# Three small edits to the routing and the last norm of a two-layer decoder kernel

## The chip, the cores and the metric

The kernel runs on one core of one Trainium2 chip. The metric is the device time in microseconds (us) of one execution; times of before and after are medians of several executions. A core has five engines that run side by side, each through its own queue in order: TensorE (PE; PEld is its weight load), VectorE (DVE), ScalarE (ACT), GpSimd (POOL) and SyncE (SP). DMA transfers are issued from the queues of SP, ACT and POOL.

## The reference, cut to what matters

Two decoder layers over 16 batches of 128 tokens with 512 features: a state-space scan, cross-attention, a ternary feed-forward, ternary self-attention, a gated cross-attention, and a mixture of experts. Each sub-layer is added to its input and normed:

```
x = _layernorm(x + _L1_xattn_ref(x, ctx_2048, ...))
x = _layernorm(x + _L1_ffn_ref(x, ...))
```

The change lies in the last one. For each token the router computes softmax scores over 64 sub-experts and keeps the top 8; these lie in 8 groups of 8. For each group with a chosen sub-expert, the token gets a mix of the group's mask vectors added, goes through the group's gate, up and down projections, and the result is scaled by the sum of its weights in the group and added up over the groups:

```
xg = x[:, None, :] + einsum('ngi,ghi->ngh', soft, mask_up_w)
a = silu(einsum('ngh,gih->ngi', xg, gate_proj_w)) * einsum('ngh,gih->ngi', xg, up_proj_w)
y = einsum('ng,ngh->nh', scalar, einsum('ngi,ghi->ngh', a, down_proj_w))
```

## The kernel before, in words

Five stages follow one another: the scan, cross-attention, feed-forward, attention (self and gated) and the experts. Tokens are held on chip as 16 tiles k.x[b] of 128 x 512.

**Order of the work.** The code is written with the Tile layer: it traces instructions in the order in which the Python code runs, and a planner then fixes each engine's queue. It goes by written order, but lets an instruction move ahead as soon as, in its own estimate of times, its inputs and its buffer are ready. On the chip a queue is then run in order: an instruction that waits holds all behind it. `k.tc.keep_in_program_order(ins)` ties an instruction behind the one that was traced just before it on the same engine; it holds back that instruction only. A tile with a tag shares its tag's buffers: with bufs=4, the fifth one waits until the first has been read for the last time.

**Routing.** `Moe.route(p)` routes the pair of batches 2p and 2p+1. It is a generator whose pieces (up to each `yield`) are set between other work by `tick()`, twice in each step of the loop. In order: transpose x (L1413), copy to r_x (L1415), scores (L1420), softmax (L1427), top 8, sorting by group through a matmul with `sel` (L1449), group sums `scal`, exponentials r_ex (L1460), counts by matmul (L1467); then places, and the routing rows. A row is 776 numbers a token: 512 of x (the copy in L1476, on ACT), 256 of the group weights (L1498 and L1499, on DVE), 8 of `scal` (L1500). Rows have four buffers, two pairs' worth. Then `scatter` stores each row to DRAM (L1507, on SP) and sends it to the buckets of its groups with indirect DMAs (L1509, on POOL), two in each step: 16 for a pair of the first half, 14 for one of the second. Batches 0 to 7 (pairs 0 to 3) are routed within the gated attention, pairs 4 to 7 from the third step of the expert stage on.

**Experts.** `stage_moe` runs over 98 units: two halves, 8 groups, 6 tiles of 128 bucket rows each, and for the last group of the second half the 8 batches 8 to 15 themselves. In step t the loop fetches the row of unit t+5 (L1519, SP), and for its neighbours makes the weights' transpose (places: pts, soft), the mask sum xg (L1546, L1548), its transpose (turn_in: ptx L377 through transpose4, copy L1554 on ACT), the gate and up projections (L1562, activation L1565 on ACT, product L1566 on DVE), the transpose of act (L1572, L1574), the down projection (L1579), and the store of the result (L1589, DMA from ACT's queue in L1590). `combine` gathers results back (L1598) and adds them to x (L1605) on POOL. The weights of a group and its mask matrix mup (L1381 to L1391) are loaded ahead.

**The end.** For the last group, `store` adds y to x[b] (L1584); after each odd b it calls `finish(b - 1)`, which norms both batches with one call of `layernorm` (L62): statistics L68 and L69 for each, one chain of eleven small DVE steps for both (`rsqrt`, L53 to L58), a scaling for each (L72), and two stores to DRAM (L1617, SP).

Of the kernel before, what the change touches and what calls it, by code (L numbers as in the profile page):

```python
# [10 lines left out]
F32 = mybir.dt.float32  # L11
# [9 lines left out]
P = 128  # L21
NB = 16
D = 512
# [38 lines left out]
def layernorm(k, ins, outs, eps=1e-5, keep=lambda ins: ins):  # L62

    nc, n = k.nc, len(ins)
    mv = k.small.tile([P, n, 2], F32, tag=f"ln_mv{n}", name="ln_mv")
    for i, r in enumerate(ins):
        st = k.small.tile([P, nc.vector.BN_STATS_DIM], F32, tag="ln_st", name="ln_st")
        keep(nc.vector.bn_stats(st, r))  # L68
        keep(nc.vector.bn_aggr(mv[:, i, :], st))  # L69
    rstd = rsqrt(k, mv[:, :, 1], n, eps, keep=keep)  # L70
    for i, (r, o) in enumerate(zip(ins, outs)):
        keep(nc.vector.tensor_scalar(o, r, mv[:, i, 0:1], rstd[:, i : i + 1], ALU.subtract, ALU.mult))  # L72
# [656 lines left out]
def stage_ffn(k):  # L729
# [4 lines left out]
    with ExitStack() as ctx:  # L734
# [24 lines left out]
        for n, sn in enumerate(states):  # L759
            nxt = prepare(states[n + 1]) if n + 1 < len(states) else iter(())  # L760
            for i, x in enumerate(sn.xs):
                st = sn.step[:, i : i + 1]
                po = po_.tile([P, D], F32, tag="po", name="po")
                for h in range(HB):
# [24 lines left out]
                    if n and h >= 2:  # L789
                        next(ahead, None)  # L790
                nc.vector.tensor_tensor(x, po, x, ALU.add)
            late = finish(sn)
        for _ in late:
            pass
# [520 lines left out]
class Moe:  # L1315
# [90 lines left out]
    def route(self, p):  # L1406

        k, nc, wr, E, NG = self.k, self.nc, self.wr, self.E, self.NG
        half, xs = p // (NB // 4), k.x[2 * p : 2 * p + 2]
# [38 lines left out]
        for i in range(2):  # L1448
            nc.tensor.matmul(pf[:, i], wT[:, i * P : (i + 1) * P], self.sel, start=True, stop=True)  # L1449
        yield  # L1450
        rows = [wr.tile([P, self.ROW], F32, tag="r_row", name="r_row", bufs=4) for _ in range(2)]
        scal = wr.tile([P, 2, NG], F32, tag="r_sc", name="r_sc", bufs=2)
        ind = wr.tile([P, 2, NG], F32, tag="r_in", name="r_in", bufs=2)
        indb = wr.tile([P, 2, NG], BF16, tag="r_ib", name="r_ib", bufs=2)
# [17 lines left out]
        nc.vector.tensor_scalar(s16, s16, 1e-30, None, ALU.max)  # L1472
        nc.vector.reciprocal(s16, s16)
        nc.vector.tensor_tensor(e3, e3, s16.unsqueeze(2).to_broadcast([P, 2 * NG, self.GS]), ALU.mult)
        for x, row in zip(xs, rows):
            nc.scalar.copy(row[:, 0:D], x)  # L1476
        yield
        pos = wr.tile([P, 2, NG], F32, tag="r_po", name="r_po", bufs=2)
        for i in range(2):
            off = wr.tile([P, NG], F32, tag=f"r_off{half}", name="r_off", bufs=2)  # L1480
# [100 lines left out]
    def store(self, u):  # L1581
        if u.to is None:
            b, k = u.b, self.k
            self.nc.vector.tensor_tensor(k.x[b], u.y, k.x[b], ALU.add)  # L1584
            if b % 2:
                self.finish(b - 1)
            return
        y = self.wk.tile([P, D], F32, tag="yo", name="yo", bufs=3)
        self.nc.vector.tensor_copy(y, u.y)  # L1589
        self.nc.scalar.dma_start(u.to, y)  # L1590
# [19 lines left out]
                yield  # L1610
            self.finish(b - 1, k.tc.keep_in_program_order)

    def finish(self, b, keep=lambda ins: ins):
        xs = self.k.x[b : b + 2]
        layernorm(self.k, xs, xs, keep=keep)
        for i, x in enumerate(xs):
            self.nc.sync.dma_start(self.k.args["out"][b + i], x)  # L1617
# [210 lines left out]
```

## Time and profile before

| | us |
|---|---|
| median of 3 executions | 3327.35 (3319.4 to 3329.7) |
| the profiled execution | 3324.17 |
| its span, first to last instruction | 3322.3 |
| PE busy in the span | 3145.9 (95%) |
| DVE, POOL, ACT busy | 1872.8, 1388.4, 1379.3 |
| mean granted TensorE clock | 0.972 of full speed |

The profile gives each instruction of one execution with its engine, line, start and duration. "Idle before" is the time that the engine stood before an instruction, with what it waited for last. The view by stretches gives the busy time of each engine between two times; the view of waits sums who waited for whom (in total, times, longest); the view of a tile lists the instructions that touch it, and what they waited for. A row of the timeline with x2 or more merges neighbours of one form.

### The profile page before, as it was taken

To read this page: it belongs to the slowest core of one execution; us is meant where nothing else is said; L and a number is where in the kernel's file an instruction comes from. 1 tells how busy PE (TensorE), PEld (TensorE's weight loads), DVE (VectorE), ACT (ScalarE), POOL (GpSimd) and SP (SyncE) were. 2 spreads that over 40 slices of the span, in tenths; PEclk is the share of its full clock that TensorE was granted. 3 is DMA by queue.
4 is the path that set the end of the run, shared out by engine and by line. 5 is a ranking of instruction groups with operands and counts; after the bars stand their busy time and mean duration, and the time that the engine had idled before them with its cause. 6 is when DMAs were issued, how large, how long until landed. Compare 5 with 4: busy or idle time off the path is not lost. (4 is left out here: it accounts for less than half of the span.)

```text
span 3322.3 us, 38519 instructions
## 1 busy us (share of the span) xinstructions
PE 3145.9 (95%) x12894; PEld 1811.7 (55%) x12944; DVE 1872.8 (56%) x4202; ACT 1379.3 (42%) x3299; POOL 1388.4 (42%) x1196
## 2 busy tenths in 40 slices
PE   6899998899999999999999989999999999999998
PEld 3444544455555555555566555666655566666665
DVE  5887878556556556556486669765553232233224
ACT  4655555233233233234433379865643231122221
POOL 6978887233333333332100066226624455333331
PEclk8999999999999999999999989999899999999999
DMA  7533332690000000001300010014435566555441
GB/s 235 134 81 97 85 85 69 227 310 8 7 4 4 7 4 4 7 0 76 112 1 1 29 36 1 11 58 150 149 115 185 193 222 210 167 180 175 160 160 62
DMA packets 162577, 317.29 MB, mean 96 GB/s; under 512 B 20233, under 2 KB 83209, under 8 KB 159300
## 3 DMA queue, kind: packets, MB, share of 16 engines
q1 hardware_dynamic: 124164, 216.23, 21.0%
q0 software_dynamic: 19200, 64.18, 5.6%
q10 hardware_dynamic: 19008, 34.35, 2.7%
q8 instruction: 105, 1.72, 0.2%
q14 instruction: 100, 0.82, 0.1%
HBM read 238.80 MB, written 129.04 MB: 111 GB/s over the span
## 5 line engine op out<-in xcount | busy, mean ns | idle before, releaser
L245 POOL TENSOR_TENSOR dBx<-dtx,BC 128x1024 f32<-128x1024 f32 x128 | 301.9, 2379 | 33.3 <-DVE h L258 26.0
L1562 PE MATMUL pg<-gu,xgT 128*128 128x352 f32 x784 | 299.4, 464 | 1.4 <-ACT act L1565 1.4
L1562 PE MATMUL pu<-gu,xgT 128*128 128x352 f32 x784 | 298.6, 463 | 0.1
L1566 DVE SCALAR_TENSOR_TENSOR act<-pu,row,act 128x352 f32<-128x352 f32 x98 | 57.1, 582 | 383.9 <-PE pu L1562 336.1
L1579 PE MATMUL y<-dn,aT 128*128 128x512 f32 x588 | 268.3, 592 | 0.0
L585 POOL TENSOR_TENSOR pr<-pr,sm 128x512 f32<-128x512 f32 x128 | 134.5, 1051 | 289.5 <-DVE sm L584 235.1
L236 ACT ACTIVATE h<-dt,negA 128x254 f32<-128x254 f32 x512 | 239.8, 474 | 14.9 <-DVE dt L178 2.1
L1605 POOL TENSOR_TENSOR x<-got,x 128x512 f32<-128x512 f32 x120 | 152.1, 1273 | 217.2 <-DMA got<-results,gidx 216.8
L616 PE MATMUL po<-w,aT 128*128 128x512 f32 x512 | 230.6, 593 | 0.5 <-DVE aT L610 0.5
L493 PE MATMUL pq<-w,xT 128*128 128x512 f32 x512 | 228.9, 594 | 0.0
L470 POOL TENSOR_TENSOR m<-m,m 128x512 f32<-128x512 f32 x96 | 121.4, 1265 | 245.3 <-DVE m L465 245.3
L1598 POOL DMA_INDIRECT got<-results,gidx x120 | 116.0, 966 | 253.0 <-DMA results<-yo 183.6
L578 ACT ACTIVATE pr<-sc,mx,sf 128x256 f32<-128x256 f32 x256 | 142.6, 561 | 188.1 <-DVE mx L571 175.8
L258 DVE TENSOR_TENSOR_SCAN h<-h,dBx 128x1024 f32<-128x1024 f32 x80 | 183.2, 2294 | 57.6 <-ACT h L236 43.0
L267 PE MATMUL py<-hC,ident 128*128 128x512 f32 x320 | 166.9, 650 | 41.2 <-ACT y L272 36.2
L1562 PEld LDWEIGHTS pu<-gu,xgT 128*128 128x128 f32 x784 | 150.3, 192 | 84.1 <-issue 2.4
L1562 PEld LDWEIGHTS pg<-gu,xgT 128*128 128x128 f32 x784 | 142.8, 192 | 65.8 <-issue 2.8
L1565 ACT ACTIVATE act<-pg 128x352 f32<-128x352 f32 x98 | 45.4, 464 | 299.6 <-PE pg L1562 278.6
L1579 PEld LDWEIGHTS y<-dn,aT 128*128 128x128 f32 x588 | 104.1, 190 | 100.8 <-issue 94.2
L1554 ACT COPY xgT<-ptx 128x512 f32<-128x512 f32 x98 | 57.3, 586 | 230.3 <-PE ptx L377 221.1
L1589 DVE COPY yo<-y 128x512 f32<-128x512 f32 x90 | 62.1, 690 | 156.7 <-PE y L1579 145.7
L493 PEld LDWEIGHTS pq<-w,xT 128*128 128x128 f32 x512 | 93.5, 190 | 102.0 <-issue 99.0
(363 smaller groups left out, 6830.5 us busy)
## 6 DMA issues: line engine op xcount, KB each, us to landing
bucket<-zeros SPq DMA_DIRECT2D x96, 388.0 KB, 8.2
row<-bucket SPq DMA_DIRECT2D x90, 388.0 KB, 3.5
BC<-bcd SPq DMA_DIRECT2D x128, 256.0 KB, 4.9
results<-yo ACTq DMA_DIRECT2D x90, 256.0 KB, 3.2
gu<-in_moe_guT SPq DMA_DIRECT2D x16, 1408.0 KB, 7.4
cT<-in_ctxT SPq DMA_DIRECT2D x32, 256.0 KB, 6.0
dn<-in_moe_downT SPq DMA_DIRECT2D x16, 512.0 KB, 6.8
rows<-r_row SPq DMA_DIRECT2D x16, 388.0 KB, 3.0
```

The lines of the kernel that those rows point to most:

```text
L236: nc.scalar.activation(h[:, c, :, 1:], st.dt[:, c].rearrange("p (b t) -> p b t", b=BQ)[:, :, 1:], AF.Exp, scale=negA[:, c, n : n + 1])
L245: nc.gpsimd.tensor_tensor(dBx, st.dtx, BC[:, 0].unsqueeze(1).to_broadcast([P, KC, TQ]), ALU.mult)
L258: nc.vector.tensor_tensor_scan(hf, hf, df, 0.0, ALU.mult, ALU.add)
L267: nc.tensor.matmul(st.py[c], k.ident, st.hC[n][:, 2 * c : 2 * c + 2], start=n == 0, stop=n == NS - 1)
L470: nc.gpsimd.tensor_tensor(m1, m1, m2, ALU.add)
L493: nc.tensor.matmul(ps, src[:, c], w[c], start=c == 0, stop=c == KC - 1)
L578: nc.scalar.activation(pr[:, j], st.sc[g, i][:, j], AF.Exp, scale=st.sf[:, h : h + 1], bias=st.mx[g, i][:, j : j + 1], accum_out=sm[:, j : ...
L585: nc.gpsimd.tensor_tensor(pr, pr, sm.unsqueeze(2).to_broadcast([P, 2, 2 * P]), ALU.mult)
L616: nc.tensor.matmul(st.po, aT[:, j], k.wo[h // 8][:, h % 8], start=h == 0, stop=h == G * J - 1)
L1562: nc.tensor.matmul(ps, u.xT[:, c], gu[:, c, lo : lo + I], start=c == 0, stop=c == KC - 1)
L1579: self.nc.tensor.matmul(u.y, u.aT[:, c], u.w[1][:, c], start=c == 0, stop=c == 2)
L1605: nc.gpsimd.tensor_tensor(k.x[b], got, k.x[b], ALU.add)
```

## The change

The rows are taken from their pool in the last piece of `route` instead of the third from last; the two copies of x into them are written in that last piece too, behind the `yield` that stood after them, and each is kept in its written place on ACT. The last two batches, 14 and 15, are normed and stored one by one.

```diff
@@ route
-        rows = [wr.tile([P, self.ROW], F32, tag="r_row", name="r_row", bufs=4) for _ in range(2)]
         scal = wr.tile([P, 2, NG], F32, tag="r_sc", name="r_sc", bufs=2)
...
         nc.vector.tensor_tensor(e3, e3, s16.unsqueeze(2).to_broadcast([P, 2 * NG, self.GS]), ALU.mult)
+        yield
+        rows = [wr.tile([P, self.ROW], F32, tag="r_row", name="r_row", bufs=4) for _ in range(2)]
         for x, row in zip(xs, rows):
-            nc.scalar.copy(row[:, 0:D], x)
-        yield
+            k.tc.keep_in_program_order(nc.scalar.copy(row[:, 0:D], x))
         pos = wr.tile([P, 2, NG], F32, tag="r_po", name="r_po", bufs=2)
@@ store
             self.nc.vector.tensor_tensor(k.x[b], u.y, k.x[b], ALU.add)
-            if b % 2:
+            if b >= NB - 2:
+                self.finish(b, n=1)
+            elif b % 2:
                 self.finish(b - 1)
@@ finish
-    def finish(self, b, keep=lambda ins: ins):
-        xs = self.k.x[b : b + 2]
+    def finish(self, b, keep=lambda ins: ins, n=2):
+        xs = self.k.x[b : b + n]
```

## The prediction, made before the change was run

> **What bounds the kernel now.** I read the page's busy times first (TensorE busy 95% of the span), then the busy time of each engine by stage. Columns of a row below: stretch, its length, then PE, PEld, DVE, ACT and POOL busy, the granted clock, DMA share, GB/s. The three stretches are the end of the attention stage, the first routed part of the expert stage, and the rest of it.
>
> ```profile
> 2180.00:2440.00 260.00, 239.60 (x1573) 154.99 (x1572) 156.23 (x521) 167.00 (x516) 131.45 (x126) 0.91 0.31 110
> 2440.00:2660.00 220.00, 205.59 (x815) 127.47 (x816) 80.62 (x203) 64.46 (x129) 83.00 (x77) 0.97 0.55 187
> 2660.00:3300.00 640.00, 640.00 (x2374) 390.19 (x2373) 182.65 (x391) 137.32 (x312) 243.83 (x223) 1.00 0.51 171
> ```
>
> From 2660 us on TensorE has no gap and the full clock, so whatever TensorE loses earlier in this stage moves the end one for one. Between 2440 and 2660 us it loses 14.4 us, and more to the clock. Next I asked the waits of TensorE from 2420 us on, and the view of the tile r_row (the routing rows):
>
> ```profile
> PE ptx L377 <- DVE xg L1548: 9.6, 3, 4.8
> PE pts L1540 <- DMA row<-bucket: 2.5, 3, 1.3
> ```
>
> ```profile
> L1476 ACT COPY r_row<-x x16: 601/618/621, 2190.8 to 2631.7; 128x512 f32<-128x512 f32 x16
> ...
>   DMA bucket<-r_row,r_to: 34.5, 4
> ...
>   DVE x L72: 18.4, 6
> ```
>
> ACT stands still at the copy into a routing row ten times: four times, 34.5 us, until a scatter has read the row buffer that it wants, six times, 18.4 us, until the norm has written x. The timeline shows what the first kind does to TensorE (start, duration, engine, line; idle before in brackets):
>
> ```profile
> 2549.49 0.97 POOL L1509 DMA_INDIRECT bucket<-r_row,r_to  x1 [0.30 <-issue]
> ...
> 2551.39 0.62 ACT L1476 COPY r_row<-x 128x512 f32<-128x512 f32 x1 [9.51 <-DMA bucket<-r_row,r_to]
> 2551.91 0.46 ACT L1565 ACTIVATE act<-pg 128x352 f32<-128x352 f32 x1
> ...
> 2552.91 0.68 DVE L1548 TENSOR_TENSOR xg<-pm,row 128x512 f32<-128x512 f32 x1
> ...
> 2553.73 0.71 PE L377 MATMUL ptx<-ident,xg 128*128 128x128 f32 x4 [4.32 <-DVE xg L1548]
> ...
> 2554.23 1.38 PE L1562 MATMUL pg<-gu,xgT 128*128 128x352 f32 x2
> ...
> 2557.67 0.76 PE L1562 MATMUL pu<-gu,xgT 128*128 128x352 f32 x2
> ```
>
> The row to see is the ACT copy: the activation of the unit (L1565) is queued behind it, DVE's product L1566 and sum L1548 behind that, and TensorE, out of work, idles 4.32 us. Then a pair of matmuls takes 1.38 us instead of 0.76 until 2557.67. The wait table names DVE; the cause is two steps back, on ACT. The second such place:
>
> ```profile
> 2631.72 0.62 ACT L1476 COPY r_row<-x 128x512 f32<-128x512 f32 x1 [11.29 <-DMA bucket<-r_row,r_to]
> ...
> 2634.06 1.09 PE L377 MATMUL ptx<-ident,xg 128*128 128x128 f32 x4 [4.78 <-DVE xg L1548]
> ```
>
> The other two waits (7.79 and 5.90 us) fit into ACT's slack but for 0.72 us of TensorE at 2618.93.
>
> **Part 1, copies kept in their written place: the expert stage.** The two waiting pairs are batches 12 to 15. Their copies sit in ACT's queue some 110 us ahead of the rest of their routing step: the exact part of a row (L1499) is written at 2669.06 and 2730.55. In their written place they come just before that. The buffers they need were last read by scatters issued at 2559.67 and 2628.58 that landed by 2563 and 2632, so they are free by about 100 us: no wait. Gone are 4.32 + 4.78 + 0.72 = 9.8 us of idle TensorE, and the slow matmuls. A pair of matmuls at full clock is 0.59 us from the next (2557.67 to 2558.26; the row's 0.76 overlaps it). First place: three pairs from 2554.23 to 2557.67 take 3.44 instead of 3 x 0.59 = 1.77, 1.7 lost. Second: from 2634.06 to 2639.57, 5.5 us, for four transposes (0.45 at full clock) and four pairs (2.36), 2.7 lost. Together 4.4, and the sum is 14.2 us. The Trainium skill (TensorE: Matmul & The Clock Gate, What's actually happening) has the clock halved after an idle window of about 3.4 us and restored after about 3.4 us of work: that would make 1.7 per stall, 3.4 in all, and 13.2 us. The second row shows a slow stretch of 5.5 us, so I take 14.2.
>
> What is late next: without the block, L1565 follows its matmuls at once and leaves ACT 3.5 us idle before it, as in every undisturbed unit (pitch 8.42 us); nothing else in that stretch is late by more than the 2.5 us of row fetches at 2458 to 2468, which stay. Ends: 12 to 16.
>
> What moves with the copies: they are 16 x 0.62 us on ACT. In the expert stage eight of them (batches 8 to 15) land in ACT's 3.5 us gaps: nothing; without that cover, 2 x 0.52 a routing step, 4 us. Each hangs behind the ACT instruction written before it, mostly the issue of a results store, which waits for DVE's yo; queued behind are only the next unit's ACT steps, 3.5 us away. The row's store on SP and its scatters on POOL need copy and L1499. POOL takes up the scatters of these four steps 10, 4.8, 4.7 and 5.7 us after L1499, so the copy has that long. SP's fetches behind a row store run five units (42 us) ahead. Cost 0.
>
> **Part 1 in the attention stage.** Here the copies of batches 0 to 11 follow the norm at once. Where TensorE feels it: at 2194.18 it waits 1.41 us for at_T (L1042), queued behind two copies, and at 2234.95 1.69 us for at_T behind a copy that had waited 2.31 for the norm. Together some 3 us. At the longest ACT wait (7.89 us to 2279.36) TensorE's three waits name DVE, and DVE stood behind its own wait of 5.50 us for POOL's x (L1232): no gain there. Against it: eight of these copies now fall into the middle of other exps, 8 x 0.52 = 4.2 us of an ACT that is busy 167 of 260 us; I charge about a third of it, 1.3. The order of the whole stage is planned anew around the moved copies. Net gain 2, ends from a gain of 8 (half the 18.4 us turned into TensorE time) to a loss of 6 (all 4.2 us on the path and one slow-clock stretch of 1.7).
>
> Taking the rows later, after the yield, moves no instruction but the row's own writes (L1498 to L1500), which come later than that place anyway, but for L1500, by 3 to 5 us of no consequence: nobody waits for it before L1499. Cost 0; at worst it rides with the copy.
>
> **Part 2, the last two batches.** After the last matmul everything is DVE:
>
> ```profile
> 3309.01 0.16 DVE L56 TENSOR_TENSOR rs_t<-rs_y 128x2 f32<-128x2 f32 x1
> 3309.09 0.69 DVE L1584 TENSOR_TENSOR x<-y,x 128x512 f32<-128x512 f32 x1
> ...
> 3311.53 0.68 DVE L1584 TENSOR_TENSOR x<-y,x 128x512 f32<-128x512 f32 x1
> ...
> 3313.19 0.17 DVE L53 TENSOR_SCALAR rs_a<-ln_mv 128x2 f32<-128x2 f32 x1
> ...
> 3315.36 1.00 DVE L72 TENSOR_SCALAR x<-x,ln_mv,rs_y 128x512 f32<-128x512 f32 x2
> ```
>
> Batch 15 is added at 3311.53; stats and aggregate to 3313.19; eleven small steps, 2.17 us, to 3315.36; two scalings to 3316.36; two stores, the second landing behind the first. Batch 14 was added at 3309.09 and waited for 15. Now 14 gets eleven steps of its own and 15's end carries one scaling less (0.5). The Trainium skill (VectorE: DVE Perf Modes, The DRAIN you can't avoid) speaks against this: the next step starts only when the pipeline is empty, so keep the count of steps low. At the dependent pitch of 0.195 us that is 11 x 0.195 = 2.1 more, less 0.5: 1.6 slower. But the first two rows show a step that doesn't depend on the one before it starting 0.08 later, so 14's steps fit between 15's. Three of them start before 3311.53; the other eight and 14's scaling cost some 0.7 that the gaps don't hide: last scaling ends 0.2 later. The last store then runs alone: stores land in 2.2 to 3.1 us here, I take 0.7 off. Net gain 0.5; ends: gain 1.2 (all in gaps), loss 2.3 (14 wholly ahead of 15).
>
> **Sum.** 14.2 + 2 + 0.5 = 16.7 off a span of 3322.3, 3305.6; with the 1.9 us around it (3324.17 - 3322.3), 3307.5 against 3324.17. The median, 3327.35, lies 3.2 above that execution: 3310.5.
>
> **Rivals.** (a) *The gain goes back into a new order (14 in 100).* The planner fills the freed ACT queue with another early instruction that waits: ACT already waits 12.3 us in five places for the load of mup (L1385), up to 4.0 each. For: it is the same kind. Against: those fit in the 3.5 us slack now. If two of them cost as much as the first stall now (4.3 + 1.7 = 6 us): 3322.5. (b) *The attention stage gains too (12 in 100).* The 18.4 us were felt by half, and its slow clock (0.91) recovers: 8 instead of 2, and 2 more of clock: 3302.5. Against: the waits there name DVE. (c) *Slower (6 in 100).* POOL at the third and fourth routing steps takes up the scatters 0.56 us after L1499 (2337.07, 2337.63; 2377.47, 2378.03). A copy queued late behind exps on ACT would hold POOL there, and with it the attention norms (L1206) and x behind it; the longest such wait now is 5.8. Four steps at 5.8 and a slow clock of 1.7 each make 30 us, less 14.7: 3343. It is slower on balance from 3.7 us a step. Against: ACT has slack, and the copy's input is long ready. (d) That nothing changes would need the 34.5 us to be no cause of TensorE's stalls; the chain of starts 2551.39, 2551.91, 2552.91, 2553.73 leaves no room for that.
>
> **Chances.** Likeliest, 68 in 100, 3303 to 3317; (b) 12, (a) 14, (c) 6. The runs before spread over 10 us, so 0.3% (10 us) is about what can be told from no change: faster by more 0.79, within 0.15, slower 0.06. Range 3300 to 3319: the likeliest case, (b), and the nearer edge of (a).
>
> **What would show it.** Right: no ACT wait for a scatter at L1476; the PE wait for xg down to about 0.5 us; PE busy near 220 of 220 less the 4 to 5 us at the stage's start; copies within 5 us before L1499. Wrong: a new ACT wait in the expert stage, POOL waiting for r_row from ACT, or an attention stage longer by several us. The tail is right if 15's scaling ends within 5.5 us of the last matmul.

## The result, and the profile after

| | before | after |
|---|---|---|
| median of 6 executions each, one comparison | 3328.11 (3319.40 to 3336.66) | 3304.88 (3301.27 to 3308.06) |
| the profiled execution, its span | 3324.17, 3322.3 | 3305.51, 3303.3 |
| mean granted TensorE clock | 0.972 | 0.976 |

The ratio is 0.9934, with a 95% interval of 0.9918 to 0.9950: 23.2 us faster between the medians, 19.0 between the spans. The forecast was 3310.5. Its main term came out nearly as worked out; a second one was some two and a half to four times too small.

First the busy time by stretch, as before the change (length, then PE, PEld, DVE, ACT and POOL busy, granted clock, DMA share, GB/s):

```profile
2180.00:2440.00 260.00, 241.13 (x1620) 156.18 (x1619) 161.67 (x556) 168.33 (x519) 133.63 (x128) 0.94 0.33 113
2440.00:2660.00 220.00, 215.90 (x869) 133.58 (x868) 86.88 (x220) 70.98 (x138) 91.00 (x85) 0.99 0.61 201
2660.00:3290.00 630.00, 630.00 (x2331) 383.64 (x2330) 176.98 (x372) 133.43 (x304) 234.59 (x214) 1.00 0.51 169
```

Two different things have happened. In the second row TensorE stands idle 4.1 us instead of 14.4, and its clock went from 0.97 to 0.99. In the first row the idle time is almost what it was, 18.9 us after 20.4, and yet more matmuls fit into the same 260 us (1620 after 1573), because the clock went from 0.91 to 0.94. The trace holds the clock itself, which is either 1.00 or 0.50: TensorE was at half clock for 47.8 of these 260 us before and for 30.7 after, which is up to 8.5 us of lost time less. The expert stage got back the time of its stalls and of the slow clock behind them; the attention stage got back time of slow clock alone.

TensorE's waits from 2400 us on (in total, times, longest):

```profile
PE pts L377 <- DVE at_T L1044: 4.0, 1, 4.0
PE pts L1540 <- DMA row<-bucket: 1.8, 3, 0.8
PE pg L1562 <- ACT act L1565: 1.4, 1, 1.4
PE ptx L377 <- DVE xg L1548: 0.5, 1, 0.5
```

The wait for xg is down from 9.6 us to 0.5. The view of the tile r_row says why:

```profile
L1477 ACT COPY r_row<-x x16: 612/621/650, 2246.4 to 2717.4; 128x512 f32<-128x512 f32 x16
...
  ACT at_s L1198: 6.4, 1
```

Before, the copies ran from 2190.8 to 2631.7 us; now they run from 2246.4 to 2717.4. The two lines on idle ACT, for a scatter (34.5 us) and for the norm (18.4 us), are gone. What is left is one wait of POOL, 6.4 us, that names ACT. That looks like rival (c), a late copy that holds POOL. The timeline of that place clears it (DVE, ACT and POOL rows of the same kernel):

```profile
2374.87 0.62 ACT L1477 COPY r_row<-x 128x512 f32<-128x512 f32 x1
...
2376.32 0.49 DVE L1499 TENSOR_TENSOR r_row<-r_ex,r_row 128x128 fp32r<-128x128 f32 x2
...
2377.37 1.01 POOL L1509 DMA_INDIRECT bucket<-r_row,r_to  x1 [6.37 <-ACT at_s L1198]
```

The copy ends at 2375.49, the row's exact part at 2376.81, and the scatter follows 0.56 us after that, as it did before (2377.47, 2378.03, after a wait of 5.82). POOL waits for DVE; the exp on ACT that is named merely ended just then. The copy costs nothing there.

The end, with 14 and 15 normed apart:

```profile
3292.86 0.15 DVE L53 TENSOR_SCALAR rs_a<-ln_mv 128x1 f32<-128x1 f32 x1
3292.93 0.68 DVE L1584 TENSOR_TENSOR x<-y,x 128x512 f32<-128x512 f32 x1
...
3294.85 0.28 DVE L56 TENSOR_TENSOR rs_t<-rs_y 128x1 f32<-128x1 f32 x2
3295.04 0.28 DVE L57 SCALAR_TENSOR_TENSOR rs_t<-rs_t,rs_a 128x1 f32<-128x1 f32 x2
...
3296.01 0.54 DVE L72 TENSOR_SCALAR x<-x,ln_mv,rs_y 128x512 f32<-128x512 f32 x1
3297.05 0.55 DVE L72 TENSOR_SCALAR x<-x,ln_mv,rs_y 128x512 f32<-128x512 f32 x1
```

Batch 14's chain begins (3292.86) just as batch 15 is added (3292.93), and the small steps of the two chains lie between each other: the pairs of steps (x2) start 0.19 us apart, no further than the single steps before. The last scaling ends at 3297.60, 5.13 us after the last matmul; before it was 5.22.

### The profile page after: what moved, and what is told of

Its sections match the earlier page's. It is cut to its first block, busy times and chain, and to the rows that moved or that the text cites. A ratio compares the mean times of both kernels' runs of the same rounds, so it can differ in the third digit from the quotient of the medians.

```text
span 3303.3 us, 38574 instructions
## 1 busy us (share of the span) xinstructions
PE 3138.6 (95%) x12944; PEld 1804.4 (55%) x12944; DVE 1876.6 (57%) x4213; ACT 1379.7 (42%) x3299; POOL 1387.5 (42%) x1196
## 4 chain that ended last, share of the span: by engine, by line
PE 68%; DVE 8%; ACT 3%; POOL 1%; issue 1%; DMA 1%; SPq 0%; POOLq 0%; ACTq 0%; DVEq 0%
PE y L1579 7%; PE pu L1562 7%; PE pg L1562 7%; PE pq L493 7%; PE po L616 6%; PE po L783 4%; PE pk L493 3%; PE sc L565 3%; PE ao L605 3%; PE pt L377 3%; PE pv L493 3%; PE ps L1144 2%; PE pu L769 2%; PE pg L769 2%; PE pT L593 1%; PE ptx L377 1%
## 5 line engine op out<-in xcount | busy, mean ns | idle before, releaser
L245 POOL TENSOR_TENSOR dBx<-dtx,BC 128x1024 f32<-128x1024 f32 x128 | 301.7, 2376 | 34.5 <-DVE h L258 27.5
```

Source lines behind the costliest of these rows:

```text
L245: nc.gpsimd.tensor_tensor(dBx, st.dtx, BC[:, 0].unsqueeze(1).to_broadcast([P, KC, TQ]), ALU.mult)
```

## The experiments

The theory: the gain of the expert stage comes from the tie alone, which keeps the copies of batches 12 to 15 from standing in ACT's queue for a buffer that is not free. The rivals: the gain comes from taking rows and writing the copy later, from scarce row buffers, from the tail, or from the attention stage. Each profile gives two stage lengths: the attention stage with routing (first scores of the gated attention to first gate projection of the experts) and the expert stage (first gate projection to last y). "Ratio" is to the kernel before in the same comparison, with its 95% interval; before's median was 3328.11 beside the change, 3328.30 beside e1 to e4, 3324.25 beside e5 to e8 and 3328.14 beside e9 to e12.

| kernel | attention | experts | median | ratio |
|---|---|---|---|---|
| before | 331.7 | 864.8 | 3328.11 | |
| after | 324.8 | 849.8 | 3304.88 | 0.9934 (0.9918 to 0.9950) |
| e1 tail only | 332.5 | 864.6 | 3327.69 | 0.9999 (0.9987 to 1.0010) |
| e2 routing only | 331.1 | 849.7 | 3306.15 | 0.9930 (0.9908 to 0.9953) |
| e3 later, no tie | 332.1 | 866.0 | 3327.05 | 1.0000 (0.9991 to 1.0009) |
| e4 tie only | 334.5 | 850.3 | 3311.70 | 0.9949 (0.9930 to 0.9968) |
| e5 the change again | 324.2 | 849.4 | 3304.21 | 0.9938 (0.9924 to 0.9952) |
| e6 late half tied | 335.3 | 850.0 | 3314.53 | 0.9964 (0.9951 to 0.9977) |
| e7 early half tied | 327.9 | 864.5 | 3317.02 | 0.9975 (0.9964 to 0.9985) |
| e8 change, x on DVE | 305.8 | 849.5 | 3289.22 | 0.9900 (0.9881 to 0.9919) |
| e9 change, two rows | 322.4 | 850.5 | 3304.69 | 0.9938 (0.9923 to 0.9952) |
| e10 before, x on DVE | 318.3 | 867.3 | 3312.75 | 0.9954 (0.9938 to 0.9970) |
| e11 before, filler | 334.3 | 864.8 | 3323.47 | 0.9988 (0.9980 to 0.9995) |
| e12 e8, other turns | 311.2 | 852.2 | 3292.93 | 0.9904 (0.9889 to 0.9918) |

### e1 and e2: the two parts apart

e1 is the kernel before with the tail's edit alone:

```diff
-            if b % 2:
+            if b >= NB - 2:
+                self.finish(b, n=1)
+            elif b % 2:
                 self.finish(b - 1)
```

> The kernel before with the change of the last two batches alone. My account (routing carries the gain, the tail some 0.4 us): median within 3 us of the kernel before, four ACT waits for a scatter at the row copies still there (about 34 us), last scaling ends 5.1 us after the last matmul as against 5.2. Rival (the tail carries several us of the 23): 3318 to 3322 us.

e2 is the change without that edit; its diff is the `route` part of the change.

> The change without its last part: batches 14 and 15 normed as a pair. My account: like the full change within 1 us, 3305 to 3306, with no ACT wait for a scatter. Rival (tail carries several us): 3309 or more.

The tail alone can't be told from no change (12 executions against 23). The routing alone is as fast as the whole change (4 executions, 3299.67 to 3311.59). All that can be measured comes from the routing part.

### e3 and e4: the later place and the tie apart

e3 has everything but the tie; e4 has the tie alone, in the old place, rows taken early:

```diff
 e3, against the change
-            k.tc.keep_in_program_order(nc.scalar.copy(row[:, 0:D], x))
+            nc.scalar.copy(row[:, 0:D], x)
 e4, against before
-            nc.scalar.copy(row[:, 0:D], x)
+            k.tc.keep_in_program_order(nc.scalar.copy(row[:, 0:D], x))
```

> The full change but the copies are not tied to their place: rows are taken and copied in the last piece of route, free to move. My account (the tie does it, since x is ready long before and a free copy is moved ahead as before): near the kernel before, 3324 to 3329, ACT waits for a scatter 30 us or more, PE wait for xg near 9 us. Rival (taking the rows later is enough): near the full change, 3303 to 3308, no such wait.

> The kernel before with the two copies tied in the place where they stood, one piece of route earlier, rows taken where they were. My account: the same as the full change but for the tail, 3304 to 3308, no ACT wait for a scatter. Rival (place and late taking matter beside the tie): at least 5 us above that, with a wait for the row buffer or for x at the copies.

e3's median lies 1.2 us from before's, its ratio at 1.0000. Its view of r_row, the lines on the copies:

```profile
L1477 ACT COPY r_row<-x x16: 601/618/621, 2193.8 to 2637.5; 128x512 f32<-128x512 f32 x16
...
  DMA bucket<-r_row,r_to: 33.0, 4
...
  DVE x L72: 10.5, 6
```

The source has the copies last, and the planner still puts them first: the last one is done by 2638, and the wait for the scatters is back, four times. Where a copy is written decides nothing as long as it may move; the tie decides. ACT's and POOL's order of instructions in e3 is that of the kernel before. TensorE's order is the same in e3 as in the change, and the expert stage differs by 16.2 us: the stall doesn't come from TensorE's own queue. The recorded waits for a scatter stand in ACT's.

e4 confirms it from the other side: the tie alone takes the expert stage to 850.3. But e4 as a whole misses what was expected of it (3304 to 3308): it stays 6.8 us above the change (5.5 above e2 in the same comparison), with an attention stage of 334.5. The rival's sign didn't come, since ACT waits neither for a row buffer nor for x at the copies. The intervals of the ratios overlap a little, so the size is not sure; it seems that the later place, worthless by itself, is worth something once the copies are tied, and that in the attention stage.

### e5, e6 and e7: which half of the copies

e5 is the change again; e6 and e7 are the change with only half of the copies tied:

```diff
-            k.tc.keep_in_program_order(nc.scalar.copy(row[:, 0:D], x))
+            ins = nc.scalar.copy(row[:, 0:D], x)
+            if p >= NB // 4:        # e6; in e7: p < NB // 4
+                k.tc.keep_in_program_order(ins)
```

> The changed kernel once more, for a second profile. In the first, the expert stage (first gate projection to last down projection) took 849.8 us as against 864.8 before, and the attention stage (first gated scores to that first gate projection) 324.8 as against 331.7. My account: expert stage 850 again. For the attention stage, if the change gains there: 325 to 327; if the first profile was a lucky execution: 330 to 332.

> The full change, but only the copies of batches 8 to 15 (routed in the expert stage) are tied; those of batches 0 to 7 move freely. My account: the expert stage's 15 us are all there (stage of 850), no ACT wait for a scatter; the waits for the norm's x at batches 0 to 7 stay. Median 3307 to 3313, by how much the attention stage gains. Rival (the early copies' waits for x carry half the gain): 3316 or more.

> The counterpart: only the copies of batches 0 to 7 are tied. My account: four ACT waits for a scatter (about 33 us) and the 865 us of the expert stage are back; median 3322 to 3327, the distance to the kernel before being what the attention stage gains. Rival as in the run before: 3316 or less.

On this chip before has a median of 3324.25 (15 executions) and the change 3304.21: 20.0 us less. e6 lies 9.7 below before, e7 7.2; together 16.9, so most of the gain is the sum of the halves. Each gains in its own stage: e6 has the short expert stage (850.0, 14.8 less than before's) and an attention stage 3.6 us longer than before's in its profile; e7 the long expert stage (864.5, with ACT waiting for scatters 34.7 us, four times) and an attention stage 3.8 us shorter in its profile. Both medians miss what was expected of them: e6 was put at 3307 to 3313 and is 3314.53, e7 was put at 3322 to 3327 and is 3317.02. Both misses lie in the attention stage: it counts for more than I had it, e6 lost time there and e7 gained it.

In that stage e6's TensorE is no more idle than before's: 240.05 us busy of 260 (2180 to 2440 us), at a granted clock of 0.89 instead of 0.91. So its longer stage is clock too.

### What the clock does in the attention stage

One place, from a pair of routing steps, in the kernel before (PE rows of the timeline):

```profile
2373.24 0.30 PE L377 MATMUL pts<-ident,at_s 128*128 128x128 f32 x1 [1.13 <-DVE r_in L1456]
2375.06 0.17 PE L1467 MATMUL pc<-r_ib,trib 128*128 128x16 bf16 x1 [1.52 <-DVE r_on L1462]
...
2378.11 2.07 PE L1183 MATMUL sc<-kT,qT 32*128 32x128 f32 x14
2380.11 5.36 PE L1228 MATMUL pw<-x_wo,oT 128*128 128x512 f32 x8
```

and after:

```profile
2372.03 0.30 PE L377 MATMUL pts<-ident,at_s 128*128 128x128 f32 x1 [0.54 <-DVE r_in L1455]
2373.78 0.17 PE L1466 MATMUL pc<-r_ib,trib 128*128 128x16 bf16 x1 [1.45 <-DVE r_on L1461]
...
2376.15 1.15 PE L1183 MATMUL sc<-kT,qT 32*128 32x128 f32 x14
2377.23 3.70 PE L1228 MATMUL pw<-x_wo,oT 128*128 128x512 f32 x8
```

The two gaps differ by 0.66 us in sum (2.65 against 1.99). But behind them the same 14 score matmuls take 2.07 us against 1.15, and the same eight output matmuls 5.36 against 3.70. From one gate product (L1231) to the next this place takes 21.7 us before, at a clock of 0.84, and 17.9 after, at 1.00. The clock, not the gap, makes up most of the 3.8 us: before, TensorE was at half clock from 2376.7 to 2383.5 us, after, nowhere in this place.

The same holds at two more places: one near 2222 to 2242 us takes 20.9 us at 0.92 before, with a gap of 1.69 us, and 17.7 at 1.00 after; one near 2184 to 2204 takes 18.7 at 0.91 and 17.3 at 1.00. The three together are 1.4 + 3.2 + 3.8 = 8.4 us; the stage as a whole gained 6.9, so some 1.5 is lost elsewhere in it. A candidate is TensorE's wait for at_T near the end of the stage, the 4.0 us in the table above, which was 2.5 before. The second place is steady: 17.7 us in every profile with the early copies tied and x on POOL (after, e2, e4, e5, e7, e9), 20.9 to 21.1 in the profiles of before, e1, e3 and e6, and 22.7 in e11, where they aren't. The others are not. e1 has nearly the same two gaps as before at the place shown, and goes through it at 1.00 in 18.7 us:

```profile
2381.27 0.17 PE L1467 MATMUL pc<-r_ib,trib 128*128 128x16 bf16 x1 [1.52 <-DVE r_on L1462]
...
2383.64 1.15 PE L1183 MATMUL sc<-kT,qT 32*128 32x128 f32 x14
```

(The other gap, before 2379.45, is 1.27 us.) e2 has the change's code in this stage and its order on all four engines, and loses its clock at the first place (0.82), after a gap of 2.06 us; its stage is 331.1 us long, the change's 324.8. So one profile of the attention stage can be off by several us, and the medians are the better measure.

How much of the differences is clock can be counted over all profiles. If half of the time at half clock is taken off, the attention stage is 304.4 us before and 306.0 after: counted so, it gained nothing apart from its clock. In the eleven profiles with x on POOL it then lies between 301.9 and 308.1, where the lengths themselves run from 322.4 to 335.3.

The Trainium skill (TensorE: Matmul & The Clock Gate, What's actually happening) has the clock fall after an idle window of about 3.4 us. Here, at the place shown, it fell where no single gap was above 1.6 us, and not each time. The length agrees: in all 14 traces the half-clock stretches, but for the first and the last of a trace, are whole multiples of 3.41 us on one grid of that step. What decides can be narrowed by cutting each trace from 2100 to 3290 us along its grid. At full clock, a step in which TensorE was busy for 75% or more was never followed by half clock (4461 steps); one in which it was busy for under 40% always was (54). Between the two it went both ways, 51 to half clock and 91 not.

### e9: are the row buffers scarce?

```diff
-        rows = [wr.tile([P, self.ROW], F32, tag="r_row", name="r_row", bufs=4) for _ in range(2)]
+        rows = [wr.tile([P, self.ROW], F32, tag="r_row", name="r_row", bufs=2) for _ in range(2)]
```

> The full change with two row buffers instead of four. My account: in their written place the copies meet a pair's scatters that ended 20 to 30 us earlier in the expert stage, so the buffers are not what is scarce: expert stage 850 us, no ACT wait for a scatter there, median within 5 us of the full change (3304 to 3309); at most a short wait at the fourth routing step. Rival (the change frees buffers, and four are just enough): ACT waits for scatters come back and the expert stage grows towards 865.

With half the buffers the change keeps all of its time (3304.69, in 4 executions from 3303.86 to 3305.62), and ACT has no wait for a scatter. Each engine's queue has the change's order here. For copies in their written place two buffers are enough; it was the copies that came some 100 us too early. The opposite, more buffers for the kernel before, wasn't tried.

### e11: work in the gap

Twelve transposes are put into the kernel before ahead of the counts of pair 3, to fill the second gap of the place shown:

```diff
-        pc = self.pp.tile([P, 2, 2, NG], F32, tag="pp", name="pc")
+        full = self.pp.tile([P, D], F32, tag="pp", name="pc")
+        pc = full[:, 0 : 4 * NG].rearrange("p (a b c) -> p a b c", a=2, b=2)
+        if p == 3:
+            for _ in range(12):
+                nc.tensor.transpose(full[:, P : 2 * P], k.ident, k.ident)
```

> The kernel before with 12 transposes of the identity, whose result is not used, set into TensorE's 1.5 us gap before the count matmuls of the fourth routing step (at 2375 us before). In the profiles the stretch after this gap runs at half clock where the gap is as long as in the kernel before (21.7 us for the unit pair), and at full clock where it is some 0.6 us shorter (17.7). Clock account: the pair takes 18 to 19 us, granted clock 1.00 in it, total 2 to 4 us below the kernel before. Rival (the order of the copies makes the difference, the clock is a symptom): 21 us or more, total unchanged or 1 us above.

```profile
2383.16 1.53 PE L1469 MATMUL pc<-ident 128*128 128x128 f32 x12 [1.52 <-DVE r_on L1462]
...
2387.52 3.70 PE L1228 MATMUL pw<-x_wo,oT 128*128 128x512 f32 x8
```

It didn't fill the gap: the transposes waited the same 1.52 us and ran after it. So it doesn't test the gap. Yet the clock was full behind them, the place took 20.0 us with 1.4 us of added work in it, and the median is 4.7 us lower than before's (3323.47, 17 executions, against 3328.14, 22). Added work that pays for itself would fit a clock that depends on how densely TensorE was used just before. But e1 kept its clock at this place without the transposes, and e11's profile, one of its slower executions (3329.22), has an attention stage of 334.3, longer than before's. So where the 4.7 us come from isn't shown.

### e8, e10 and e12: what holds the attention stage

With the copies gone, DVE still waits there for POOL's addition to x. The line in the table of DVE's waits, 2180 to 2440 us, before and then after:

```profile
DVE ln_st L68 <- POOL x L1232: 18.2, 7, 5.5
```

```profile
DVE ln_st L68 <- POOL x L1232: 12.7, 6, 4.1
```

The difference between the two rows is not the change's: e1, whose attention stage has before's order, has 12.8 there, and e7, with the early copies tied, 18.3. POOL's queue holds the scatters ahead of that addition, 0.97 us each and 0.30 to the next. e8 is the change with the addition on DVE; e10 is before with it; e12 is e8 with a third instead of half of the at_T copies on DVE, the rest on ACT:

```diff
-        nc.gpsimd.tensor_tensor(self.xs[i], self.xs[i], gt, ALU.add)
+        nc.vector.tensor_tensor(self.xs[i], self.xs[i], gt, ALU.add)
 e12 as well
-    DVE_TURNS = 2
+    DVE_TURNS = 3
```

> The full change, and in the gated attention the addition of the gated output to x moves from POOL to DVE. POOL's scatters hold that addition up, and DVE's norm waits for it (18.2 us in seven places before). If POOL bounds the end of the attention stage: 5 to 12 us below the full change, 3293 to 3300, and no DVE wait for x from POOL. If DVE bounds it, 16 more additions of 0.69 us on DVE make it 3305 to 3316.

> The kernel before, with only the addition of the gated output to x moved from POOL to DVE. The run with both edits was 15 us below the full change. If that gain is one of the attention stage alone: 3308 to 3312 here, the expert stage at 865 with its four waits for a scatter (33 us). Rival (it needs the copies out of the way, since ACT would now be next): 3318 or more.

> The full change, the addition to x on DVE, and in the gated attention only every third copy of transposed scores on DVE (ACT takes the others) instead of every second. If DVE is now what bounds that stage: 3282 to 3288; if ACT, 3290 to 3300.

e8 by stretch:

```profile
2180.00:2440.00 260.00, 246.53 (x1674) 159.71 (x1674) 177.00 (x578) 169.84 (x521) 116.91 (x114) 0.97 0.35 123
```

The wait is gone, TensorE is idle 13.5 us instead of 18.9, and the clock is 0.97 instead of 0.94. e8 is 15.0 us faster than the change on the same chip (3289.22 against 3304.21), more than the 5 to 12 expected, and the fastest of all. e10 gains about the same without the change, 15.4 (3312.75 against 3328.14; 3308 to 3312 was expected), all of it in the attention stage: its ACT waits for scatters 34.2 us and its expert stage stays long. So the two gains add up: 20.0 and 15.4, and e8 lies 35.0 below before. Of the 19.0 us by which e8's attention stage is shorter than the change's in their profiles, the time at half clock accounts for up to 12. e12 is no better than e8 (ratio 0.9904 against 0.9900): moving copies from DVE to ACT brings nothing more. Its 3292.93 lies in the range expected if ACT holds the stage, which no further run tested.

## Why the prediction was right, and where it was off

**The expert stage (14.2).** Right, in mechanism and size. The stage is 15.0 us shorter in the profile of the change, and between 849.4 and 850.5 us in all six profiles in which the late copies alone or all copies are tied and x stays on POOL, against 864.5 to 866.0 in those without. The two terms were 9.8 of idle time and 4.4 of slow clock. Measured are 10.3 of idle time, and the clock's record of before bears out the 4.4: half clock for 3.41 us behind the first stall (1.7 lost), and behind the second for 6.83 us, of which TensorE had work for the last 5.4 (2.7 lost); after, both places are at 1.00. The skill's page, taken as one window of 3.4 us a stall (13.2 in sum), fits the first stall; the second had two such windows. e3 shows that the tie is the cause, e6 that it is the tie of batches 8 to 15.

**The moved copies (0).** Right. ACT's waits show nothing new at the copy, POOL's longest wait for a row is 6.37 us instead of 5.82 and ends 0.56 us after L1499, as before. One sign that I gave was loose: the copies of the expert stage don't all come shortly before L1499. In all four of its routing steps the first copy of a pair comes 3 to 5 us after the first L1499, for example at 2591.7 us after 2588.4. At the last step POOL stood 2.5 us until the row was whole (the copy ended at 2717.47, L1500 at 2717.64, the scatter began at 2717.75). TensorE had no gap there.

**The attention stage (2).** This step failed in size, and in what it was made of. It is 6.9 us in the profile of the change; from the medians, 20.0 to 23.2 less 15.0 and 0.3 leaves 5 to 8. The sum in the prediction counted idle time given back, 3 us less 1.3 for copies among the exps, and had no term for the clock of this stage, whose 0.91 stood in the row that I showed. Measured, idle time fell by 1.5 us, and the clock gave the rest. I had used the slow clock where a stall of over 4 us preceded it, in the expert stage, and thought that gaps of 1 to 2 us don't touch it.

**Taking the rows later (0).** By itself right: e3 can't be told from before. With the tie it is part of why the change does better than e4, by 6.8 us in the medians of two comparisons. What of these is the place of the copy and what the rows' buffers, no run tells apart; e9 speaks against the buffers. In the attention stage e4 has the change's order on TensorE but another one on DVE, ACT and POOL, so the place also changed the plan.

**The tail (0.5).** Right in sign, too small to measure. DVE ends 0.1 us sooner where I had 0.2 later: the small steps of the second chain fit between the first one's wholly, and with 14's scaling they cost some 0.4 of the 0.5 saved, where I had 0.7. The section of the skill's page that I held against this part says itself that a step which isn't held back until the earlier ones have finished starts sooner, as the rows 0.08 us apart had shown; I had left that out. From the last scaling to the end of the span it is 5.70 us after 5.94, where I had taken 0.7 off the store. Together 0.3, and the profiles agree: from the last matmul to the end of the span it is 11.1 to 11.2 us in the five with 14 and 15 normed as a pair, 10.7 to 11.1 in the nine with them apart.

**The rivals.** (a) and (c) didn't come: ACT has no new wait in the place of the old one, and no routing step is longer by what (c) asked for. (b), the attention stage gains too, is nearer to what happened than the likeliest case: 3304.88 lies 5.6 from the forecast (3310.5, where the terms summed give 3310.7) and 2.4 from (b)'s 3302.5. But (b) had 8 of waits and 2 of clock, and the chip showed the shares the other way round. (d) is refuted by e3 and e6.

**Open.** What tips the clock at gaps of 1 to 2 us is settled only at the ends, above 75% and under 40% busy; nearly the same gaps went both ways (before and e1). Whether more row buffers would have freed the kernel before wasn't tried. That e6's attention stage is at 0.89 is measured, why it is lower than before's isn't.

## What to carry to other kernels

When TensorE waits for DVE, go back through the queues until an instruction waits that is not itself late by its data, here a copy on ACT that a planner had moved some 100 us ahead of its use to a buffer that a DMA still read; tying it to its written place removed the wait, with two buffers as well as with four. In a stretch where the mean granted clock is below 1, count the lost clock as part of what the gaps cost, even where each gap is short. An engine that issues many DMAs in order should not also hold a step that the norm of the next tile waits for.

## What the hardware showed that I had not expected

- Gaps of 1.13 and 1.52 us within 3 us were followed by half clock for 6.8 us in one profile (0.84 over 21.7 us); 1.27 and 1.52 us at the same place, in e1, by none (1.00).
- The clock changes only in whole steps of 3.41 us, and at full clock a step with TensorE busy for 75% or more never led to half clock (4461 cases in 14 traces, from 2100 to 3290 us).
- Two dependent chains of small DVE steps interleave without loss: two steps, one of each chain, every 0.19 us, the pitch of one chain alone.
- A row of the wait view named an exp on ACT (6.4 us) where POOL in truth took up a DVE result, 0.56 us after it, as before.
